# A macaron transformer block on one core: the order of head and tail, and where the softmax sums are scaled

## The chip, the cores and the metric

The kernel runs on one core of a Trainium2 chip. A core has five engines that work through their own instruction queues in order and wait for each other by semaphores: TensorE (PE, matrix products; the rows PEld are its weight loads), VectorE (DVE), ScalarE (ACT), GpSimd (POOL) and SyncE (SP, which here issues nearly all transfers). Matrix products write to PSUM, a small memory that VectorE and ScalarE read; everything else lies in SBUF. The metric is the device time of one execution in microseconds; of several executions the median counts.

## The reference

The input x has 4 batches of 4096 rows of 512 numbers, which makes 128 tiles of 128 rows. The block computes

```python
x = x + 0.5 * ffn(layernorm(x))
x = x + attention(layernorm(x))
x = x + 0.5 * ffn(layernorm(x))
```

ffn rounds both its input and its weight, in blocks of 32 numbers, to a six-bit grid with one scale for each block, multiplies them and adds a bias. attention is a neighbourhood attention with 16 heads of 32 numbers: each query looks at the 13 nearest keys of its sequence, with a relative position bias; the scores go through a softmax, the probabilities are multiplied with the values, and a last product (proj) follows.

## The kernel before, in words

Products are made in a split form, since fp32 operands are written as a high and a low half in fp16. One product of a 128-row tile is 12 matrix instructions of 512 columns (high times low, low times high, high times high, each over four chunks of 128; `product`, L146). In TensorE's rows the products go by the PSUM tile that they fill: pmf is a feed-forward product (two for each tile of rows, f1 and f2), pmv the values, pmqk the queries and keys (two for each item), pmo the product behind the attention. ps are the scores and pv the attention's product with the values, both many small instructions. All 128-row products share three PSUM buffers (`ps_m`, L93), so that a product can start only when the buffer of the third one before it has been read out.

An attention item is one of 128: four groups of 128 channels for each of 32 groups of 512 rows (GROUP is 4 tiles). `project_qk` makes the item's queries and keys: ScalarE writes the high halves (L369), VectorE the low halves (L373). `softmax` (L417 to L486) is a chain over three engines. VectorE adds bias and parts of the scores (L458, L461) and takes the maximum (L465), GpSimd subtracts it (L467), ScalarE takes the exponent (L469), and VectorE sums it for each query and block (L472, tile total, 16 to 18 numbers in each partition), inverts the sum (L473) and multiplies it by the constant PS = 1024 (L474; the second operand p_scale is a tile that holds 1024 everywhere). GpSimd multiplies the exponents by it (L476), ScalarE writes the high half of the probabilities p (L480, L481), GpSimd the low half (L483), and SP issues a transposing transfer into pT (L485). `attend` multiplies with the values, and ScalarE and VectorE empty pv into a ring of 1024 rows (L530, L536), with 1/PS.

A norm with rounding (`quantised_norms`, slots named by their start) is a chain as well: VectorE's statistics (L180, L181), three or four small GpSimd operations for the factors (L186 to L195), ScalarE's yq (L233), VectorE's block maxima, scale and inversion (sc, r; L239 to L244), GpSimd's multiplication (L246), ScalarE's rounding (L249), GpSimd's multiplication back (L251), ScalarE's and VectorE's halves hlq (L200, L204), and a transposing transfer into xT (L205), which the feed-forward product reads. In the long middle part one norm holds two tiles, one for f1 and one for f2; at both ends it holds one. The attention's norm (n2) has a shorter chain with hln and x2. A group's pmqk needs x2 of all its four tiles.

The order of the main part is written out by hand. Every piece of work is a Python generator that is put into a numbered slot with a rank; `run_slot` takes the pieces of a slot by rank, lets each emit instructions up to its next `yield n, rank`, and puts it into the slot n later. STEP is 7 slots, one step for each tile and for each item. In each engine's queue the instructions stand in that order. A yield of 0 would put a piece into the slot that is being run, which the loop before doesn't look at again. The setup ahead of `manual_schedule` (L769) is ordered by the framework's own scheduler instead: the load and rounding of the feed-forward weight fw, the sums of squares of the other weights, and the first EARLY norms. The 16 chunks of the qkv and proj weights (rows, 0 to 11 and 12 to 15) are then scaled, split (`put_scaled`, whl, L774 and L776) and transposed into wt (L699), one chunk every two slots from slot -9 on.

At the end `out_slot` and `second_slot` give the slots of pmo and of the second feed-forward product for the last tiles (LAST is 123). GpSimd adds the biases (`add_bias`, L565); of the last five tiles VectorE adds half of the ffn bias for those with even numbers.

Of the kernel before, what the change touches and what calls it, by code (L numbers as in the profile page):

```python
# [26 lines left out]
F32 = mybir.dt.float32  # L27
# [5 lines left out]
ALU = mybir.AluOpType  # L33
# [4 lines left out]
P = 128  # L38
# [9 lines left out]
MAXB = 18  # L48
# [11 lines left out]
PS = 1024.0  # L60
# [4 lines left out]
def macaron_kernel(  # L65
# [12 lines left out]
    nc = tc.nc  # L78
# [12 lines left out]
    const = ctx.enter_context(tc.tile_pool(name="const", bufs=1))  # L91
# [18 lines left out]

    least = const.tile([P, 2 * NB], F32, name="least")
    nc.vector.memset(least, F8_SCALE * XS * Q_EPS)
    p_scale = const.tile([P, MAXB], F32, name="p_scale")
    nc.vector.memset(p_scale, PS)
    minus_half = const.tile([P, 2], F32, name="minus_half")
    nc.gpsimd.memset(minus_half, -0.5)

# [2 lines left out]
    half_ffn_b = const.tile([P, dim], F32, name="half_ffn_b")  # L120
# [39 lines left out]
    slots = {}  # L160

    def begin(slot, stage, rank=5):
        slots.setdefault(slot, []).append((rank, stage))

    def run_slot(slot):
        for _, stage in sorted(slots.pop(slot, ()), key=lambda e: e[0]):
            for n, rank in stage:
                begin(slot + n, stage, rank)
                break

    xs, ys = {}, {}

# [41 lines left out]
    def moments(slot, t, which):  # L214
        tiles, mv = together[slot]
        if not mv:
            mv.append(sm.tile([P, 2, 2], F32, tag="mv", bufs=4, name=f"mv{slot}"))
        statistics(t, which, mv[0][:, tiles.index((t, which)), :])
# [114 lines left out]
    for g in range(NG):  # L333
        first = done
# [6 lines left out]
    n_items = n_batch * NG * KC  # L341
# [75 lines left out]
    def softmax(m):  # L417

        b, g, c = item_of(m)
        j0, j1 = group_blocks[g]  # L420
        n = j1 - j0
        t = qk.pop(m)


        ps = ps_s.tile([P, 3, 2, 256], F32, tag="s", name=f"ps{m}")
        for i in range(n):
            q0, k0 = (KN + at - g * GT for at in span(j0 + i))
            q0 -= late(j0 + i)
            u, w = divmod(i, PSB)
            for part, sides in ((0, 2), (1, 1)):  # L430
                for h in range(4):
                    rows = slice(h * D, (h + 1) * D)
                    nc.tensor.matmul(  # L433
                        ps[rows, u, :sides, w * KN : (w + 1) * KN],
                        t[rows, 0, part, q0 : q0 + QR], t[rows, 1, :sides, k0 : k0 + KN],
                        start=part == 0, stop=part == 1,
                    )

        def pieces(i, e):

            while i < e:
                u, w = divmod(i, PSB)
                whole = max((e - i) // PSB, 1) if w == 0 else 1
                f = min(e, (u + whole) * PSB)
                yield slice(u, u + whole), slice(w, w + (f - i) // whole)
                i = f

        yield 1, 9
        sf = sfp.tile([P, MAXB, KN], F32, tag="sf", name=f"sf{m}")
        s4 = sf.rearrange("p (u w) k -> p u w k", w=PSB)  # L450
        p4 = ps[:, :, :, : PSB * KN].rearrange("p u a (w k) -> p a u w k", k=KN)
        first = 1 if kind(j0) == 1 else 0
        last = n - (1 if kind(j1 - 1) == 2 else 0)
        for i, e in ((0, first), (first, last), (last, n)):
            for u, w in pieces(i, e):
                o = s4[:, u, w, :]
                bias = table[:, kind(j0 + i), c, :].unsqueeze(1).unsqueeze(1).to_broadcast(o.shape)
                nc.vector.tensor_tensor(o, p4[:, 0, u, w, :], bias, ALU.add)  # L458
        for u, w in pieces(0, n):
            o = s4[:, u, w, :]  # L460
            nc.vector.tensor_tensor(o, o, p4[:, 1, u, w, :], ALU.add)  # L461
        yield 1, 2
        s = sf[:, :n, :]
        top = sm.tile([P, MAXB], F32, tag="top", name=f"top{m}")
        nc.vector.tensor_reduce(top[:, :n], s, AX.X, ALU.max)  # L465
        yield 1, 4
        nc.gpsimd.tensor_tensor(s, s, bc(top[:, :n], KN), ALU.subtract)  # L467
        yield 1, 9
        nc.scalar.activation(s, s, AF.Exp, scale=alpha)  # L469
        yield 1, 4  # L470
        total = sm.tile([P, MAXB], F32, tag="total", name=f"total{m}")
        nc.vector.tensor_reduce(total[:, :n], s, AX.X, ALU.add)  # L472
        nc.vector.reciprocal(total[:, :n], total[:, :n])  # L473
        nc.vector.tensor_tensor(total[:, :n], total[:, :n], p_scale[:, :n], ALU.mult)  # L474
        yield 1, 4
        nc.gpsimd.tensor_tensor(s, s, bc(total[:, :n], KN), ALU.mult)  # L476
        yield 2, 8
        p = p_tile
        ph = p[:, :n, :KN]
        nc.scalar.copy(ph, s)  # L480
        nc.scalar.copy(p[:, :n, 2 * KN : KV], ph)  # L481
        yield 2, 4
        nc.gpsimd.tensor_tensor(p[:, :n, KN : 2 * KN], s, ph, ALU.subtract)  # L483
        pT = ptp.tile([P, MAXB, P], F16, tag="pT", name=f"pT{m}")
        nc.sync.dma_start_transpose(out=pT[:, :n, :], in_=p[:, :n, :].rearrange("p n k -> p (n k)"))  # L485
        probs[m] = pT  # L486
# [68 lines left out]
        nc.sync.dma_start(out=of[t * P : (t + 1) * P, :], in_=xs.pop(t))  # L555


    EARLY = 2
    STEP = 7

    F1, V, QK, SC, PV, OUT, F2 = 5, 2 * STEP + 6, 5 * STEP + 3, 6 * STEP, 8 * STEP + 3, 13 * STEP + 2, 12

    def add_bias(t, b, idle=True):
        engine = nc.gpsimd if idle else nc.vector
        engine.tensor_tensor(xs[t], xs[t], b, ALU.add)  # L565

    def one(f, *args):
        f(*args)
        return
        yield  # L570

    LAST = NT - GROUP - 1

    def out_slot(t):


        i = t - LAST
        if i >= 0:
            return (n_items - 1) * STEP + PV + 3 + i
        if i >= 1 - GROUP:  # L580
            return LAST * STEP + PV + 21 + 4 * i
        return t * STEP + OUT

    def second_slot(t):

        i = t - LAST
        if i in (-2, -1):
            return out_slot(NT - 1) + 3 + i
        return out_slot(t) + (F2 + 2 if i == -3 else F2)

    for t in range(NT):
        k = t * STEP
        begin(k - 18, one(load, t), 0)
        enlist(k - 10, t, "n1")
        if not 0 < t < EARLY:
            begin(k - 11, one(moments, k - 10, t, "n1"), 1)
        begin(k + F1, first_half(t))
        begin(k + V, values(t))
        begin(k + F1, one(add_bias, t, half_ffn_b), 8)
        at = out_slot(t)  # L600
        begin(at - 5, one(add_bias, t, after_b), 8)
        enlist(at + 2, t, "n3")
        begin(at, project_out(t, at + 2))
        begin(at + 6, one(add_bias, t, half_ffn_b, t < LAST or t % 2), 8)
        begin(second_slot(t), second_half(t))
    for slot in together:
        if slot >= EARLY * STEP - 10:
# [6 lines left out]
    for n in range(n_batch * NG):  # L614
        k = n * GROUP * STEP
        b, g = divmod(n, NG)
# [4 lines left out]
    with tc.tile_pool(name="setup", bufs=1) as sp, tc.tile_pool(name="scratch", bufs=2) as scr:  # L621
# [13 lines left out]

        sq = sp.tile([P, 5 * KC], F32, name="sq")
        first = min(slots)
        for slot in range(first, first + 2 * STEP, STEP):
            run_slot(slot)
        for t in range(EARLY):  # L640
            if t:
                moments(t * STEP - 10, t, "n1")
            for _ in quantised_norms(t * STEP - 10):
                pass
        chunks = (8, 9, 10, 11, 0, 4, 1, 5, 2, 6, 3, 7, 12, 13, 14, 15)
        for o in chunks:
            w, i = (qkv_w, o) if o < 3 * KC else (proj_w, o - 3 * KC)
            rows[o] = xp.tile([P, dim], F32, tag="x", name=f"rows{o}")
# [91 lines left out]
        for o in range(KC):  # L740
# [23 lines left out]
            nc.vector.tensor_tensor(hl[:, 1, :], fw[:, o, :], hl[:, 0, :], ALU.subtract)  # L764
            put_weights(4 * KC + o, hl)

        ctx.enter_context(tc.manual_schedule())  # L769

        def put_scaled(o):
            s = up[:, o // KC : o // KC + 1]
            hl = scr.tile([P, 2, dim], F16, tag="whl", bufs=4, name=f"whl{o}")
            nc.scalar.activation(hl[:, 0, :], rows[o], AF.Copy, scale=s)  # L774
            yield 1, 9
            nc.vector.scalar_tensor_tensor(  # L776
                hl[:, 1, :], rows[o], s, hl[:, 0, :], ALU.mult, ALU.subtract
            )
            put_weights(o, hl)
# [23 lines left out]
        def attention_bias():  # L803

            vbx = sp.tile([P, 2, KC, P], F16, name="vbx")
            nc.scalar.copy(vbx[:, 0], bc(vb, P))
            nc.vector.tensor_tensor(vbx[:, 1], bc(vb, P), vbx[:, 0], ALU.subtract)
            yield 1, 9
            pmb = ps_m.tile([P, dim], F32, tag="mm", name="pmb")
            product(pmb, lambda s, c: vbx[:, s, c, :], lambda s, c: wt[:, s, c, PO : PO + dim])  # L810
            yield 1, 9
            nc.vector.scalar_tensor_tensor(after_b, pmb, cp, after_b, ALU.mult, ALU.add)
# [39 lines left out]
                    masks[:, k : k + 1, :].to_broadcast([P, KC, KN]), ALU.mult, ALU.add,  # L852
                )

        begin(-11, one(scales), 9)
        for i, o in enumerate(chunks):
            begin(-9 + 2 * i, put_scaled(o), 9)
        begin(28, attention_bias(), 9)
        begin(26, one(put_table), 9)
        slot = first  # L860
# [48 lines left out]
```

## Time and profile before

| | us |
|---|---|
| runs, median of three | 2447.3 (2446.6, 2447.3, 2453.3) |
| profiled execution, own time | 2451.5 |
| its span, first to last instruction | 2449.7 |

| stretch of the span, us | PE busy | DVE busy | ACT busy | POOL busy | granted PE clock |
|---|---|---|---|---|---|
| 0 to 106 | 32.8 | 81.2 | 50.3 | 58.7 | 0.89 |
| 106 to 240 | 124.4 | 109.9 | 75.3 | 97.6 | 0.96 |
| 240 to 2300 | 2027.9 | 1754.6 | 1143.7 | 1736.1 | 1.00 |
| 2300 to 2400 | 80.8 | 66.6 | 40.9 | 69.3 | 0.92 |
| 2400 to 2450 | 35.4 | 28.4 | 11.6 | 25.4 | 0.84 |

The profile is of one execution. Its page gives busy times of the engines, the chain of work that ended last, and groups of equal instructions with their mean duration and the idle time ahead of them. The trace behind it can be asked for all waits, for the chain piece by piece, and for an engine's instructions in order of time. A row in order of time has the start, the duration from the first of its instructions to the end of the last, engine, line, operation, the written tile, the read tiles, and in brackets the idle time ahead with what ended it. A wait that is shorter than what TensorE has in its pipeline doesn't show as idle time; it shows as a larger distance from one start to the next.

### The profile page before, as it was taken

How to read it: one execution, taken by the hardware profiler on the slowest of the kernel's cores; microseconds unless marked ns; L12 is line 12 of the kernel's file. 1: busy time of each engine (PE TensorE's matmuls, PEld its weight loads, DVE VectorE, ACT ScalarE, POOL GpSimd, SP SyncE). 2: the span in 40 equal slices, each digit the busy share in tenths (PEclk: the TensorE clock that was granted, in tenths of full speed). 3: DMA queues.
4: the chain of work that ended last, by engine and by line, in shares of the span. 5: the costliest groups of instructions: out<-in, count | busy, mean ns of one | idle time of the engine just before them, and what ended most of it. 6: DMA issues, size and time to landing. Idle time of an engine off the chain costs nothing.

```text
span 2449.7 us, 82398 instructions
## 1 busy us (share of the span) xinstructions
PE 2301.3 (94%) x35539; PEld 1114.2 (45%) x35539; DVE 2040.6 (83%) x3590; ACT 1321.7 (54%) x2080; POOL 1987.1 (81%) x2010
## 2 busy tenths in 40 slices
PE   1699999999999999999999999999999999999976
PEld 0244444444444444444444444444444444444432
DVE  7788888888888888888888888888888888888765
ACT  4455555555555555555555555555555555555442
POOL 5677888888888888888888888888888888888665
PEclk9899999999999999999999999999999999999998
DMA  6687888777787778778877778786877877776653
GB/s 165 133 148 143 154 160 157 145 155 145 145 156 155 150 143 158 148 147 156 154 147 156 147 146 156 156 151 145 160 146 149 159 150 153 146 156 127 134 106 83
DMA packets 925702, 360.60 MB, mean 147 GB/s; under 512 B 718876, under 2 KB 889752, under 8 KB 925336
## 3 DMA queue, kind: packets, MB, share of 16 engines
q1 hardware_dynamic: 924992, 354.79, 74.3%
q8 instruction: 278, 4.55, 0.8%
q14 instruction: 88, 0.72, 0.1%
q10 hardware_dynamic: 344, 0.53, 0.1%
HBM read 110.15 MB, written 67.29 MB: 72 GB/s over the span
## 4 chain that ended last, share of the span: by engine, by line
PE 67%; DVE 17%; ACT 8%; DMA 4%; issue 3%; POOL 2%; SPq 0%; POOLq 0%; DVEq 0%; ACTq 0%
PE pmf L151 17%; PE pmqk L151 16%; PE pmo L151 12%; PE pmv L151 12%; PE ps L433 6%; DVE total L474 4%; DVE total L472 3%; PE pv L503 3%; DMA xT<-hlq 3%; ACT sf L469 3%; DVE qk L373 2%; ACT qk L369 2%; ACT ring L530 1%; DVE stn L180 1%; DVE total L473 1%
## 5 line engine op out<-in xcount | busy, mean ns | idle before, releaser
L151 PE MATMUL pmf<-wt,xT 128*128 128x512 f16 x3048 | 706.0, 382 | 41.0 <-DMA xT<-hlq 38.8
L151 PE MATMUL pmqk<-x,wt 128*128 128x512 f16 x3072 | 710.6, 381 | 7.9 <-DMA x<-hln 5.9
L151 PEld LDWEIGHTS <-xT 128*128 128x128 f16 x3048 | 297.6, 98 | 412.2 <-DMA xT<-hlq 53.7
L151 PEld LDWEIGHTS <-wt 128*128 128x128 f16 x3072 | 290.4, 98 | 347.1 <-issue 14.0
L246 POOL TENSOR_TENSOR yq<-yq,r 128x1024 f32<-128x1024 f32 (+1 forms) x141 | 246.3, 1747 | 201.9 <-DVE r L244 199.1
L151 PE MATMUL pmv<-wt,x 128*128 128x512 f16 x1536 | 352.4, 379 | 17.5 <-DVE qk L373 12.8
L151 PE MATMUL pmo<-wt,ring 128*128 128x512 f16 x1536 | 357.7, 383 | 4.3 <-issue 4.2
L310 ACT CAST vt<-pmv 128x512 f16<-128x512 f32 x128 | 74.9, 585 | 471.4 <-PE pmv L151 471.4
L565 POOL TENSOR_TENSOR x<-x,half_ffn_b 128x512 f32<-128x512 f32 x254 | 324.6, 1278 | 0.0
L275 DVE SCALAR_TENSOR_TENSOR x<-pmf,coef,x 128x512 f32<-128x512 f32 x256 | 179.6, 702 | 135.2 <-PE pmf L151 135.1
L530 ACT ACTIVATE ring<-pv 128x510 f16<-128x510 f32 (+8 forms) x224 | 82.3, 414 | 376.1 <-PE pv L503 376.1
L180 DVE BATCH_NORM_STATS2 stn<-x 128x6 f32<-128x512 f32 x384 | 265.3, 691 | 8.7
L151 PEld LDWEIGHTS <-x 128*128 128x128 f16 x1536 | 149.7, 97 | 215.3 <-issue 45.3
L251 POOL TENSOR_TENSOR yq<-q,sc 128x1024 f32<-128x1024 fp8e4 (+1 forms) x141 | 246.2, 1746 | 1.4 <-ACT q L249 1.4
L249 ACT ACTIVATE q<-yq,nudge 128x1024 fp8e4<-128x1024 f32 (+1 forms) x141 | 150.0, 1064 | 143.0 <-POOL yq L246 134.7
L151 PEld LDWEIGHTS <-ring 128*128 128x128 f16 x1536 | 140.9, 98 | 165.0 <-issue 9.7
L233 ACT ACTIVATE yq<-x,nbq,rsq 128x512 f32<-128x512 f32 x254 | 194.4, 809 | 37.7 <-POOL nbq L192 32.3
L476 POOL TENSOR_TENSOR sf<-sf,total 128x714 f32<-128x714 f32 (+2 forms) x128 | 178.6, 1395 | 37.1 <-DVE total L474 36.8
L186 POOL TENSOR_SCALAR rsq<-mv 128x2 f32<-128x2 f32 (+1 forms) x141 | 132.4, 939 | 89.8 <-DVE mv L181 88.4
L467 POOL TENSOR_TENSOR sf<-sf,top 128x714 f32<-128x714 f32 (+2 forms) x128 | 180.8, 1412 | 18.9 <-DVE top L465 18.7
L483 POOL TENSOR_TENSOR p<-sf,p 128x714 f16<-128x714 f32 (+2 forms) x128 | 192.6, 1505 | 4.2 <-ACT p L480 4.2
L458 DVE TENSOR_TENSOR sf<-ps,table 128x210 f32<-128x210 f32 (+5 forms) x288 | 126.5, 486 | 75.6 <-PE ps L433 74.9
(146 smaller groups left out, 3525.5 us busy)
## 6 DMA issues: line engine op xcount, KB each, us to landing
vs<-vd SPq DMA_DIRECT2D x144, 357.0 KB
x<-in_L_attn_x_dram SPq DMA_DIRECT2D x128, 256.0 KB
vd<-vt SPq DMA_DIRECT2D x128, 256.0 KB
out_dram<-x SPq DMA_DIRECT2D x128, 256.0 KB
vs<-vd SPq DMA_DIRECT2D x24, 378.0 KB
vs<-vd SPq DMA_DIRECT2D x24, 315.0 KB
rows<-in_L_attn_qkv_w_dram SPq DMA_DIRECT2D x12, 256.0 KB
xT<-hlq SPq DMA_TRANSPOSE x141
```

Source lines behind the costliest of these rows:

```text
L151: nc.tensor.matmul(pm, lhs(a, c), rhs(b, c), start=(n == 0), stop=(n == 3 * KC - 1))
L180: nc.vector.bn_stats(st, xs[t])
L233: nc.scalar.activation(y[:, u], xs[t], AF.Identity, bias=nb[:, u : u + 1], scale=rs[:, u : u + 1])
L246: nc.gpsimd.tensor_tensor(yb, yb, bc(r, QB), ALU.mult)
L249: nc.scalar.activation(q8, y, AF.Identity, bias=nudge, saturate=False)
L251: nc.gpsimd.tensor_tensor(yb, q8.rearrange("p u (n q) -> p (u n) q", q=QB), bc(sc, QB), ALU.mult)
L275: nc.vector.scalar_tensor_tensor(xs[t], pm, cf, xs[t], ALU.mult, ALU.add)
L433: nc.tensor.matmul(ps[rows, u, :sides, w * KN : (w + 1) * KN], t[rows, 0, part, q0 : q0 + QR], t[rows, 1, :sides, k0 : k0 + KN], start=par ...
L467: nc.gpsimd.tensor_tensor(s, s, bc(top[:, :n], KN), ALU.subtract)
L476: nc.gpsimd.tensor_tensor(s, s, bc(total[:, :n], KN), ALU.mult)
L483: nc.gpsimd.tensor_tensor(p[:, :n, KN : 2 * KN], s, ph, ALU.subtract)
L565: engine.tensor_tensor(xs[t], xs[t], b, ALU.add)
```

## The change

In the softmax, p_scale and L474 go. ScalarE multiplies total by 1/1024 right behind the sum, and VectorE inverts that. The sum comes three ranks earlier in its slot, and the inversion follows at rank 9 of the same slot, by a yield of 0, for which `run_slot` now runs a slot until nothing is left in it. In VectorE's queue the order sum, inversion, multiplication, low half of the queries, low half of the keys becomes sum, low half of the queries, inversion, low half of the keys. In ScalarE's queue the scaling stands between the two yq of the norm and the high half of the keys.

At the start three norms instead of two are made in the setup, and the second and third behind the feed-forward weight's code; the proj weights (12 to 15) come before those of the queries and keys, and the chunks' slots are spread over 2 to 35; the product for the attention's bias (pmb) comes two slots later.

At the end the last five pmo stand two slots apart instead of one, the second products of tiles 119 and 120 move behind the attention product of item 126, the ffn bias of the last five tiles is always GpSimd's and stands two slots ahead of its product.

```diff
-    p_scale = const.tile([P, MAXB], F32, name="p_scale")
-    nc.vector.memset(p_scale, PS)
...
     def run_slot(slot):
-        for _, stage in sorted(slots.pop(slot, ()), key=lambda e: e[0]):
-            for n, rank in stage:
-                begin(slot + n, stage, rank)
-                break
+        while slot in slots:
+            for _, stage in sorted(slots.pop(slot), key=lambda e: e[0]):
+                for n, rank in stage:
+                    begin(slot + n, stage, rank)
+                    break
...
         nc.scalar.activation(s, s, AF.Exp, scale=alpha)
-        yield 1, 4
+        yield 1, 1
         total = sm.tile([P, MAXB], F32, tag="total", name=f"total{m}")
         nc.vector.tensor_reduce(total[:, :n], s, AX.X, ALU.add)
+        nc.scalar.mul(total[:, :n], total[:, :n], 1.0 / PS)
+        yield 0, 9
         nc.vector.reciprocal(total[:, :n], total[:, :n])
-        nc.vector.tensor_tensor(total[:, :n], total[:, :n], p_scale[:, :n], ALU.mult)
         yield 1, 4
...
-    EARLY = 2
+    EARLY = 3
...
-    def add_bias(t, b, idle=True):
-        engine = nc.gpsimd if idle else nc.vector
-        engine.tensor_tensor(xs[t], xs[t], b, ALU.add)
+    def add_bias(t, b):
+        nc.gpsimd.tensor_tensor(xs[t], xs[t], b, ALU.add)
...
         if i >= 0:
-            return (n_items - 1) * STEP + PV + 3 + i
+            return (n_items - 1) * STEP + PV + 3 + 2 * i
...
         i = t - LAST
+        if i in (-4, -3):
+            return (n_items - 1) * STEP + PV + i
         if i in (-2, -1):
             return out_slot(NT - 1) + 3 + i
-        return out_slot(t) + (F2 + 2 if i == -3 else F2)
+        return out_slot(t) + F2
...
-        begin(at + 6, one(add_bias, t, half_ffn_b, t < LAST or t % 2), 8)
+        begin(at + 6 if t < LAST else second_slot(t) - 2, one(add_bias, t, half_ffn_b), 8)
...
-        for slot in range(first, first + 2 * STEP, STEP):
+        for slot in range(first, first + EARLY * STEP, STEP):
             run_slot(slot)
-        for t in range(EARLY):
-            if t:
-                moments(t * STEP - 10, t, "n1")
-            for _ in quantised_norms(t * STEP - 10):
-                pass
-        chunks = (8, 9, 10, 11, 0, 4, 1, 5, 2, 6, 3, 7, 12, 13, 14, 15)
+        for _ in quantised_norms(-10):
+            pass
+        chunks = (8, 9, 10, 11, 12, 13, 14, 15, 0, 4, 1, 5, 2, 6, 3, 7)
...
+        for t in range(1, EARLY):
+            moments(t * STEP - 10, t, "n1")
+            for _ in quantised_norms(t * STEP - 10):
+                pass
...
-            yield 1, 9
+            yield 3, 9
             pmb = ps_m.tile([P, dim], F32, tag="mm", name="pmb")
...
-        begin(-11, one(scales), 9)
-        for i, o in enumerate(chunks):
-            begin(-9 + 2 * i, put_scaled(o), 9)
+        begin(0, one(scales), 9)
+        for slot, o in zip((2, 4, 5, 6, 10, 13, 16, 19, 21, 23, 25, 27, 29, 31, 33, 35), chunks):
+            begin(slot, put_scaled(o), 9)
```

## The prediction

> **What bounds the kernel now.** I read the page's busy shares and chain first, then the chain of waits in one repeating step, then the engines' own rows in time, then the two ends.
>
> ```profile
> PE 2301.3 (94%) x35539; PEld 1114.2 (45%) x35539; DVE 2040.6 (83%) x3590; ACT 1321.7 (54%) x2080; POOL 1987.1 (81%) x2010
> ```
>
> TensorE is busy 94% of 2449.7 us. In the stretch 240 to 2300 us it is busy 2027.9 of 2060 us, so at most 32 us lie there; in 0 to 106 it is busy 32.8 and in 2300 to 2450 116.2. What a faster VectorE is worth is bounded by these idle spaces, not by the work that VectorE is spared. One step in the chain of waits (start, us, what):
>
> ```profile
> 1016.45 0.58 ACT ring L530
> 1017.03 0.58 ACT qk L369
> 1017.61 0.22 ACT qk L382
> 1017.83 0.80 ACT sf L469
> 1018.62 0.02 issue
> 1018.65 0.91 DVE total L472
> 1019.56 0.02 issue
> 1019.58 0.28 DVE total L473
> 1019.86 0.02 issue
> 1019.88 1.12 DVE total L474
> 1021.00 0.67 DVE qk L373
> 1021.67 0.04 issue
> 1021.71 2.75 PE pmv L151 x12
> ```
>
> This is a loop across engines: the attention product pv ends, ScalarE empties it and takes the exponent, VectorE sums, inverts and scales by 1024 (L472 to L474), and only then writes the low half of q (L373), which frees the PSUM buffer for pmv. L474 handles 17 numbers per partition and takes 1.12 us. TensorE's rows in time show what this costs:
>
> ```profile
> 1018.82 2.75 PE L151 MATMUL pmf<-wt,xT 128*128 128x512 f16 x12
> 1021.71 2.75 PE L151 MATMUL pmv<-wt,x 128*128 128x512 f16 x12
> 1024.30 2.75 PE L151 MATMUL pmf<-wt,xT 128*128 128x512 f16 x12
> ```
>
> Without a wait a product starts 2.59 us after the one before it (pmv to pmf here); pmf to pmv is 2.89. Over the 110 steps of the trace that show pmf, pmv, pmf, ps whole, the distances over 2.59 add to 30.4 us for pmf to pmv and to 9.0 for pmv to the second pmf, which waits for the transposed tile xT. Nothing else repeats. The waits view, with less because it counts only full idleness, agrees in kind (us, times, longest):
>
> ```profile
> PE pmf L151 <- DMA xT<-hlq: 38.8, 17, 14.3
> ...
> PE pmv L151 <- DVE qk L373: 12.8, 57, 0.7
> ```
>
> The ends, in TensorE's rows:
>
> ```profile
> 73.79 5.30 PE L151 MATMUL pmf<-wt,xT 128*128 128x512 f16 x12 [14.31 <-DMA xT<-hlq]
> ```
> ```profile
> 2415.03 5.34 PE L151 MATMUL pmf<-wt,xT 128*128 128x512 f16 x24
> 2430.72 15.05 PE L151 MATMUL pmf<-wt,xT 128*128 128x512 f16 x60 [10.35 <-DMA xT<-hlq]
> ```
>
> **The scaling of the sums.** Removed: 128 of L474, 174 to 1302 ns, median 1124. In the quoted step it began at 1019.88 and ended as GpSimd's bias add (1019.70 + 1.27 = 20.97) ended. Added: 128 ScalarE scalings of 16 to 18 columns; the nearest row, ring 128x16, takes 191 ns. In the instruction order ScalarE runs it behind the two yq (end 1020.06) and ahead of the second high half of q, which thus moves by about 0.2 us: 1020.3 to 1020.95. VectorE now runs the sum, then the first low half at once (1019.58 to 1020.25 instead of from 1021.00), then waits about 0.1 for ScalarE, inverts (0.27), and takes the second low half from 1020.95 to 1021.65 instead of 1022.33. The first frees pmv's buffer 1.4 us earlier, 1.1 before pmf has ended; the second frees the next pmf's 2.4 before it is wanted. GpSimd's multiplication by total, which waits behind the inversion, could start at 1020.65, but GpSimd is in its bias add to 1020.97 anyway. The wait of 0.3 is gone; what is late next is xT. Its issue stands on SP behind pT's. In 17 of the 110 steps the second pmf already waits for xT (every fourth step, where a pT issue takes 4.5 to 6 us behind the stack loads vs); these steps hold 5.2 of the 30.4, and that is lost again. In some eight more xT has less than 0.35 to spare; half of their 2.6 goes. So 30.4 - 5.2 - 1.3 = 24 gained. Ends: 0, if every step then waits for xT, and 30.4 + 9.0 = 39, if pT's issue, held by GpSimd's p, also moves forward by the 0.7 that VectorE gains. I take 24, as 93 of 110 steps show no wait for xT at all.
>
> [...]
>
> **The head.** Tile 2's norm moves from the slots into the setup: VectorE gets statistics, maximum, scale and inversion ahead of the last FFN weight (0.69 + 0.18 + 0.67 + 0.2 + 0.25 = 2.0), GpSimd the factors, tile 0's bias (1.26) and a multiplication (1.05). VectorE is busy 23.3 of 25 us there, so I let the first pmf move from 52.8 to 56 (ends: 53 and 58). x2 and x3 are loaded before the transposes, which cost SP 0.6 each, hidden. Tile 2's xT (SP issue 1.23) now follows the first whl at about 55 and is there before pmf of tile 1 ends, so the gap of 14.31 goes: that pmf runs at 62.5 instead of 73.8. This is not the gain, since the next tile's norm is a chain of its own: in before, hlq of one tile to hlq of the next (68.7, 78.4, 88.4) takes about 10 us. From tile 0's add (60 instead of 61.6; VectorE is free of five whl by then) I add statistics, three GpSimd factors, yq, maximum, two multiplications, q, hlq twice: hlq of tile 4 ends near 83 to 84 instead of 89.1. The attention bias changes little: pmb stands between the same products and still waits for vbx (95.4 before, some 92 now, behind one more whl of 1.2); but VectorE's after_b, which stood 3.69 idle for pmb ahead of the next hlq, now comes behind it. The eight whl moved to slots 19 to 35 each put 0.72 on ScalarE, 0.7 to 1.25 on VectorE and 1.2 to 1.8 of SP issue into these steps, three or four a step as the steps before them had. Together the first pmqk goes from 105.8 to about 101: 5 gained. Ends: 4 lost (the setup's 3.2, and one whl more on the path), 10 gained (a whole norm step). I take 5, from the nearest rows. From 106 on TensorE is the limit again, and the delay carries over one to one.
>
> **The tail.** Before, GpSimd works through the factors of four tiles, each held by pmo's 2.59, before the first multiplication (yq at 2415.71, though its factor r was ready at 2412.9); the five xT issue from 2427.95 and five pmf follow from 2430.72. After the change GpSimd's order alternates: factors 123, bias 127, factors 124, yq 123, factors 125, and so on. Counted from 2406.74 with the rows' durations (five factor chains of 1.2, ten multiplications of 1.05, four biases of 1.27): 6 + 10.5 + 5.1 = 21.6, so the last multiplication ends near 2428.5 instead of 2433.8. The two biases that leave VectorE (1.5 each) come last on GpSimd, by 2431, before their pmf ends. hlq (0.62 + 1.05) and the 2.8 from xT's issue to its product (as from 2427.95) put the last pmf at 2433.0; its 2.6, the add 0.75 and the 3.1 from add to end give 2439.5: 10.2 gained. SP alternates xT with the outputs; an xT that waits there behind an output waits for a product already done by 2427.5. Lost: the last ring write stands behind one more add (0.67), and in the last items, where GpSimd does wait for total (2.31 at 2333, 2.67 at 2353) and L474 took only 0.18, the ScalarE hop and the low half in front cost up to 0.48 each, thrice: 2.1 together. Moving the products of tiles 119 and 120 behind pv of item 126 is costed at nothing: pv of item 127 waits for pT (5.34), whose issue GpSimd's p releases at 2394.6. Without that cover a product of 2.6 would show. So 8 gained; ends 0 and 12 (the whole gap of 10.35, and the 2.1 by which 15.05 exceeds 60 times 0.216).
>
> [...]
>
> **Sum.** 24 + 5 + 8 = 37. The profiled execution took 2451.5 (span 2449.7); 2451.5 - 37 = 2414.5. It stood 4.2 above the median of the runs, 2447.3, so I forecast 2410.
>
> **Rivals.** First, the wait only changes its name: xT, not q, ends last in most steps, since it comes by SP after pT. For it: in the chain view xT appears between steps about every 72 us. Against: 93 steps have no such wait, and half the steps have 7.5 us or more between xT's issue and its product where the late ones have 5.2. Then 24 shrinks to about 6: 2428. Second, the head loses: the added setup work and the denser whl make the early norm steps longer, and 4 is lost instead of 5 gained: 2419; for it the setup's VectorE share, against it the 14.31 gap. Third, slower: the new ScalarE hop is put where the scaling was short. Place: total between L472 and GpSimd's L476; price 0.48 a step, 128 steps, 61 us, less 13 from the ends: 2495. It decides if GpSimd, not TensorE, sets the step, that is if its idle time ahead of yq (1.67 in the step shown, waiting for r) falls to nothing. GpSimd is busy 81%; 1.67 a step speaks against it. Fourth, the removed operation was covered and the ends cancel: 2445 to 2450, against the 2.89 of pmf to pmv.
>
> **How the numbers follow.** Runs tell about 0.3% (7.3 us) from no change. Forecast 0.60 (its own range 2399 to 2420), xT 0.17, head 0.12, slower 0.06, covered 0.05. Faster: 0.60 + 0.16 + 0.12 = 0.88; same 0.06; slower 0.06. The range reaches down to 2398, where xT's 9 us come too (39 instead of 24), and up to 2434, past the xT case with a head that gains nothing; beyond lie the last two cases and a few hundredths at either end.
>
> **What would show it.** L474 gone, a 0.2 us ScalarE row on total; pmf to pmv at 2.59 in most steps and VectorE no releaser of pmv; xT's wait not above some 15 us between 240 and 2300; TensorE idle there near 8 to 10 instead of 32. The third pmf follows the second without a gap, the first pmqk near 101. The last run of five pmf broken up, the end some 9 us nearer to the last pmo than before (34.5: 2415.2 to 2449.7). I am wrong if pmv to pmf grows as pmf to pmv shrinks, if the first pmf starts past 58, or if SP holds the last xT behind an output.

## The result, and the profile after

The changed kernel takes 2461.4 us in the median (2454.0 to 2470.7, 12 runs), the kernel before 2448.6 on the same chip (2443.1 to 2453.3, 12 runs). The ratio is 1.0053, with a 95% interval of 1.004 to 1.0066: slower by 0.5%, where 2410 and a gain of 1.5% had been forecast. The profiled execution of the changed kernel took 2455.8 us, its span is 2454.0. The changed file has other line numbers: L149 is the matrix product (L151 before), L471 the sum, L472 ScalarE's scaling, L474 the inversion, L372 the low halves.

The page's busy shares of the changed kernel come first:

```profile
PE 2294.5 (94%) x35539; PEld 1116.3 (45%) x35539; DVE 1939.6 (79%) x3459; ACT 1333.7 (54%) x2208; POOL 1984.7 (81%) x2012
```

VectorE is spared 101 us, ScalarE has 128 instructions and 12 us more. The removed part itself went as forecast. VectorE's, ScalarE's and TensorE's rows in time of one step (start, us, engine, line, operation, tiles, and in brackets the idle time ahead):

```profile
1023.07 0.90 DVE L471 TENSOR_REDUCE total<-sf 128x17 f32<-128x714 f32 x1 [0.64 <-ACT sf L468]
1023.89 0.74 DVE L372 SCALAR_TENSOR_TENSOR qk<-pmqk,qk_b,qk 128x512 f16<-128x512 f32 x1
1024.62 0.27 DVE L474 RECIPROCAL total<-total 128x17 f32<-128x17 f32 x1
```
```profile
1024.39 0.20 ACT L472 ACTIVATE total<-total 128x17 f32<-128x17 f32 x1
```
```profile
1023.24 2.75 PE L149 MATMUL pmf<-wt,xT 128*128 128x512 f16 x12
1025.83 2.75 PE L149 MATMUL pmv<-wt,x 128*128 128x512 f16 x12
```

The low half stands ahead of the inversion, the scaling takes 0.20, and pmv starts 2.59 after pmf, the distance without a wait. Summed from 340 to 2300 us, the time over 2.59 between pmf and pmv falls from 29.5 us to 0.0. But TensorE's waits (us in total, times, longest) and its busy time by stage show it spent elsewhere:

```profile
PE pmf L149 <- DMA xT<-hlq: 33.8, 26, 4.3
...
PE pv L503 <- DMA pT<-p: 12.9, 2, 7.3
PE pmqk L149 <- issue: 10.4, 8, 2.4
PE ps L432 <- issue: 10.1, 4, 4.4
PE pv L503 <- issue: 9.4, 9, 1.7
```
```profile
0.00:106.00 106.00, 33.70 (x115) 13.18 (x115) 85.54 (x166) 49.74 (x97) 57.26 (x84) 0.92 0.63 152
...
240.00:2300.00 2060.00, 2011.11 (x31538) 984.28 (x31536) 1647.45 (x2911) 1150.06 (x1877) 1725.38 (x1703) 1.00 0.80 150
```

(In the second fence: stretch, its length, then busy us and instructions of PE, PEld, DVE, ACT and POOL, PE's granted clock, DMA share, GB/s.) Between 240 and 2300 TensorE is now idle for 48.9 us, where it was 32.1. The total of the xT waits looks smaller than before (38.8), but of the old total 14.3 was the gap in the head and 10.4 the one in the tail; from 340 to 2300 alone the waits for xT grew from 4.9 to 19.7. There the time that pmv to the second pmf takes over 2.59 grew from 8.3 to 23.2 us, in 21 steps, the larger ones 72 us apart or a multiple of it, at each fourth step. The other pairs of neighbours grew by another 25 us, most of which the waits call "issue" (7.8 us before, 26.4 now), idle time that waits for nothing the profile shows.

The ends, in TensorE's rows:

```profile
62.76 2.75 PE L149 MATMUL pmf<-wt,xT-3_389 128*128 128x512 f16 x12
65.35 2.75 PE L149 MATMUL pmf<-wt,xT 128*128 128x512 f16 x12
...
106.21 4.04 PE L149 MATMUL pmqk<-x,wt 128*128 128x512 f16 x18 [1.60 <-DMA x<-hln]
```
```profile
2424.93 5.34 PE L149 MATMUL pmf<-wt,xT 128*128 128x512 f16 x24
2430.99 2.76 PE L149 MATMUL pmf<-wt,xT 128*128 128x512 f16 x12 [0.72 <-DMA xT<-hlq]
2435.66 2.76 PE L149 MATMUL pmf<-wt,xT 128*128 128x512 f16 x12 [1.90 <-DMA xT<-hlq]
2440.37 9.63 PE L149 MATMUL pmf<-wt,xT 128*128 128x512 f16 x36 [1.95 <-DMA xT<-hlq]
```

The gap ahead of the third pmf is gone, yet the first pmqk starts at 106.2, as before (105.8). The last five pmf are broken up, and from the last pv to the end it takes 44.8 us (2409.2 to 2454.0) instead of 50.2. What was lost, then, lies in the steady steps.

### The profile page after: what moved, and what is told of

The parts are those of the page before. It is cut to its first block, busy times and chain, and to the rows that moved or that the text cites. A ratio compares the mean times of both kernels' runs of the same rounds, so it can differ in the third digit from the quotient of the medians.

```text
span 2454.0 us, 82265 instructions
## 1 busy us (share of the span) xinstructions
PE 2294.5 (94%) x35539; PEld 1116.3 (45%) x35539; DVE 1939.6 (79%) x3459; ACT 1333.7 (54%) x2208; POOL 1984.7 (81%) x2012
## 4 chain that ended last, share of the span: by engine, by line
PE 81%; DMA 6%; DVE 5%; ACT 3%; issue 3%; POOL 2%; SPq 0%; DVEq 0%; POOLq 0%; ACTq 0%
PE pmqk L149 24%; PE pmf L149 24%; PE pmo L149 13%; PE pmv L149 11%; PE ps L432 6%; DMA xT<-hlq 5%; PE pv L503 3%; ACT yq L232 1%; ACT qk L368 1%; ACT sf L468 1%; DVE stn L179 1%; DVE fw L749 0%; POOL rsq L188 0%; ACT ring L530 0%; DVE sf L457 0%
## 5 line engine op out<-in xcount | busy, mean ns | idle before, releaser
L149 PE MATMUL pmf<-wt,xT 128*128 128x512 f16 x3048 | 705.8, 382 | 33.9 <-DMA xT<-hlq 33.8
L149 PE MATMUL pmqk<-x,wt 128*128 128x512 f16 x3072 | 713.2, 382 | 17.4 <-issue 10.4
L149 PEld LDWEIGHTS <-xT 128*128 128x128 f16 x3048 | 297.2, 98 | 407.9 <-DMA xT<-hlq 49.0
L149 PEld LDWEIGHTS <-wt 128*128 128x128 f16 x3072 | 291.0, 98 | 358.0 <-issue 27.6
L149 PE MATMUL pmo<-wt,ring 128*128 128x512 f16 x1536 | 359.1, 384 | 5.2 <-issue 5.1
L149 PE MATMUL pmv<-wt,x 128*128 128x512 f16 x1536 | 354.9, 381 | 5.1 <-DVE mvn L180 5.1
L149 PEld LDWEIGHTS <-x 128*128 128x128 f16 x1536 | 150.7, 98 | 188.4 <-DMA x<-hln 5.6
L372 DVE SCALAR_TENSOR_TENSOR qk<-pmqk,qk_b,qk 128x512 f16<-128x512 f32 x256 | 190.9, 746 | 43.4 <-ACT qk L368 42.7
L149 PEld LDWEIGHTS <-ring 128*128 128x128 f16 x1536 | 141.1, 98 | 166.4 <-issue 10.6
```

The costliest lines, as they stand in the source:

```text
L149: nc.tensor.matmul(pm, lhs(a, c), rhs(b, c), start=(n == 0), stop=(n == 3 * KC - 1))
L372: nc.vector.scalar_tensor_tensor(t[:, s, 1, KN:], pms[s], bias, t[:, s, 0, KN:], ALU.add, ALU.subtract)
```

## The experiments

Each run is compared with runs of the kernel before on the same chip, so that the time of the kernel before differs a little from group to group. Four runs took the parts one by one and tried the suspect that the trace offered: every fourth step the second pair's stack loads (vs) stand on SP directly ahead of an output, an x load, pT and xT, and there pT's issue took 5.2 us before and 6.3 after.

**The scaling alone** (head and tail of before; `run_slot` as in the change):

```diff
-    p_scale = const.tile([P, MAXB], F32, name="p_scale")
-    nc.vector.memset(p_scale, PS)
...
-        yield 1, 4
+        yield 1, 1
         total = ...
         nc.vector.tensor_reduce(total[:, :n], s, AX.X, ALU.add)
+        nc.scalar.mul(total[:, :n], total[:, :n], 1.0 / PS)
+        yield 0, 9
         nc.vector.reciprocal(total[:, :n], total[:, :n])
-        nc.vector.tensor_tensor(total[:, :n], total[:, :n], p_scale[:, :n], ALU.mult)
```

> The scaling part alone, with head and tail of before. Theory A (the wait for the low halves goes, and its 27 us come back as waits for xT and as instructions that TensorE issues late, because DMA and not VectorE sets the pace of a step): the time is 8 to 14 us over before, 2455 to 2463, with no wait pmv<-DVE qk, pmf<-DMA xT some 25 to 35 us in 340-2300 and over 20 us of idle time that waits for nothing. Theory B (the scaling gains its 24 us and it is the new head that puts the steps out of phase with the transfers): 2420 to 2430, with pmf<-DMA xT near the 17 us of before.

Measured: 2467.9 against 2448.3, ratio 1.0084 (1.0055 to 1.0113). It is slower alone than with the other parts, and theory B, which blamed the head, falls. The time is a little past theory A's range.

**The head alone and the tail alone** (the diff's other two parts).

> The head part alone: three tiles ahead of the loop, the new order of weight chunks, the scales at slot 0. Theory A: the head is worth -4 to +2 us, as the start of the 12th step showed (347.5 to 343.4), so 2443 to 2451, and the steady steps keep the 27 us of pmv<-DVE qk. Theory B: the head alone makes it slower by 20 us or more, 2468 to 2480, with longer waits for xT in 340-2300.

> The tail part alone: the last products out and halves in their new slots. Both theories: nothing changes before 2300 us, and from the last pv to the end 5 us less (50.2 to about 45), so 2443 to 2446. If the new slots of the last outputs hold up SP's queue for the last items, the 2 to 4 us that after lost between items 120 and 127 are in it too, and the time is 2446 to 2450.

Measured: the head 2451.5, ratio 1.0015 (1.0001 to 1.0029), at the upper end of theory A's range; the tail 2445.6, ratio 0.9985 (0.9972 to 0.9998), in the first range. The head gains nothing, the tail some 3 to 4 us.

**The stack loads four slots later, in the changed kernel and in the one before.**

```diff
-        begin(k + 8 * STEP, one(load_stack, b, g, 1), 9)
+        begin(k + 8 * STEP + 4, one(load_stack, b, g, 1), 9)
```

> After, with the loads of the second pair's stack issued four slots later (slot 60 of each group in place of 56), so that they no longer stand on SP ahead of an output, an x load and the transposes pT and xT. Theory A in its narrow form (those loads are what makes xT late): the wait pmf<-DMA xT falls from 33.8 to under 15 us and the time by 15 to 25, to 2431 to 2446. Theory A in its wide form (any transfer's bytes delay the instructions that TensorE fetches): xT's wait falls but issue stalls stay at or above 30 us, and the time is 2446 to 2456. Theory B: no difference from after, 2455 to 2465.

> Before, with only the second pair's stack loads moved from slot 56 to slot 60 of each group. If the collision on SP every fourth step costs the kernel whether or not TensorE waits for VectorE, the 8.2 us of pmv-to-pmf excess in 340-2300 go, the 27 us of pmv<-DVE qk stay, and the time is 2425 to 2440. If it costs only where the scaling has made TensorE arrive earlier, the time is 2444 to 2452.

Measured: changed kernel 2415.1, ratio to before 0.9863 (0.984 to 0.9887); kernel before 2436.8, ratio 0.9949 (0.993 to 0.9967). The first lies below all its ranges, the second in its first range. In the changed kernel pmv to pmf from 340 to 2300 fell from 23.2 to 0.0 us over its 2.59. So those loads are where most of the loss is. At their old place they cost the changed kernel 46 us and the kernel before 11; why four times as much, these runs don't say.

**The order without ScalarE, and another way to free the low half.** In the first the sum, low half and inversion stand in the new order, but the multiplication by p_scale stays on VectorE, behind the inversion (`run_slot` again as in the change). In the second the old kernel's low half goes ahead of the sum:

```diff
-        yield 1, 4
+        yield 1, 1
         total = ...
         nc.vector.tensor_reduce(total[:, :n], s, AX.X, ALU.add)
+        yield 0, 9
         nc.vector.reciprocal(total[:, :n], total[:, :n])
         nc.vector.tensor_tensor(total[:, :n], total[:, :n], p_scale[:, :n], ALU.mult)
```
```diff
-        yield 1, 6
+        yield 1, 3
         put_low(0)
```

> Before, with the order of the scaling part (reduce, low half, reciprocal) but with the multiply kept on VectorE behind the reciprocal and no work for ScalarE. If the order alone frees the low half, pmv<-DVE qk is gone as in the scaling alone and the time is within 6 us of it, 2455 to 2472. If it was the multiply's 0.2 us on VectorE that counted, the wait stays over 15 us and the time is 2444 to 2452.

> Before, with the query's low half put ahead of the reduce of the sums on VectorE and nothing else moved: the wait pmv<-DVE qk goes, but the probabilities and so the transpose pT come 0.5 to 0.8 us later instead of earlier. If any earlier arrival of TensorE is given back at the fourth steps, the time is 2448 to 2468, with pmf<-DMA xT over 25 us in 340-2300. If it is pT's earlier start into the stack loads that costs, as the scaling part brings it, this keeps half or more of the 27 us: 2422 to 2436.

Measured: the order alone 2416.1, ratio 0.9863 (0.9834 to 0.9892), the low half first 2424.1, ratio 0.9887 (0.9864 to 0.991). The first misses both ranges by 28 us and more, and with it theory A in its general form fell: with the wait for the low half gone, the gain was not given back. The second lies in its second range, but the reason given there, that pT's earlier start costs, does not stand: in the mean of the fourth steps pT starts 5.3 us behind the loads in the first, which gains, and in the scaling alone, which loses. What remained between 2416 and 2468 was ScalarE's instruction in place of VectorE's, and the rows of both kernels did not bear that out: VectorE's and GpSimd's work stood at the same places within the step, and pT's issue started at the same moment (9.9 us after pmv in the mean of some 27 fourth steps) but took 6.2 us with ScalarE's scaling and 5.3 without.

**Scaling and tail, without the new head.**

> Scaling and tail without the new head, the stack loads in their old slot 56. If the head of the change is worth -4 to +4 us when the scaling is in too, the time is within 5 us of after, 2453 to 2466. If the new head is what kept after from being slower still (the scaling alone stood at 2468), it is 2462 to 2472.

Measured: 2470.0, ratio 1.0073 (1.0048 to 1.0099), the second range. The new head is not the cause of the loss: without it the kernel is no faster (2470.0 against 2461.4 with it). Whether the 8 us between the two are the head's is not shown, as the intervals of the two ratios overlap.

**What else had gone: the tile.** Every kernel so far that was slower than before by more than 0.3% lacked p_scale; every faster one had it, but for the changed kernel with the later loads. p_scale is 72 bytes in each partition, laid out as 96, near the start of the memory; without it every later tile lies 96 bytes lower. In the built programs of before and after the stack vs starts at 204288 and 204192, that is at 798 times 256 and 96 bytes below it; the x tiles (65792, 65696) and pT (195072, 194976) also left a multiple of 256. Four runs tested this as theory C, against the instruction itself (theory D):

```diff
+    p_scale = const.tile([P, MAXB], F32, name="p_scale")
+    nc.vector.memset(p_scale, PS)
```

in after; the same in after with the later stack loads; the same in the scaling alone; and in the kernel before

```diff
     nc.vector.memset(p_scale, PS)
+    shift = const.tile([P, 40], F32, name="shift")
+    nc.vector.memset(shift, 0.0)
```

> After, with the constant tile p_scale kept in its place, written once and read by nothing. Theory C (taking out those 72 bytes, 96 as they are laid out, moves every later tile 96 bytes down, off the 256-byte boundaries on which x, vs and pT stood, and their transfers take longer): all the loss goes, pT's issue at the fourth steps falls from 6.3 to about 5.3 us, and the time is 2400 to 2418, the forecast of 2410 in it. Theory D (it is ScalarE's hop itself that delays): no difference from after, 2455 to 2465. [...]

> Before, with an unused constant tile of 160 bytes behind p_scale, so that all later tiles lie 160 bytes higher, which is the same place within 256 bytes as 96 lower. Theory C: the transfers lengthen as in after, and before loses what lies beyond its 27 us of waits for VectorE and more, 2465 to 2495, with pT's issue at the fourth steps near 6 us. Theory D: 2444 to 2452.

> After with the tile kept and the second pair's stack loads at slot 60. Theory C: both remove waits for the same transposes, so the gains do not add up; what is left of waits for xT goes, and the time is 2390 to 2410. Theory D: as with the loads moved alone, 2411 to 2419.

> The scaling part alone with the tile kept. Theory C: 24 us under before as forecast for it, give or take 10, 2414 to 2434, against 2468 without the tile. Theory D: 2460 to 2476.

Measured, all against 2446.5 for the kernel before: after with the tile 2407.1, ratio 0.9847 (0.9827 to 0.9866); before shifted 2488.2, ratio 1.0171 (1.0155 to 1.0186); after with the tile and later loads 2389.1, ratio 0.9769 (0.9755 to 0.9783), just under its range; the scaling alone with the tile 2416.5, ratio 0.988 (0.986 to 0.9901). All four went theory C's way; theory D is out. An unused tile of 72 bytes is worth some 50 us in after (54 by the medians, 50 by the ratios, 1.0053 against 0.9847), and 160 unused bytes cost before 42. The later loads are worth 18 us with the tile (2407.1 to 2389.1), against 46 without it. With the loads moved and the tile gone some 25 us are still lost (2415.1 against 2389.1), so the loss is not in that one collision alone. The multiplication on ScalarE (2416.5) is worth no more than the order alone with VectorE's (2416.1).

SP's rows in time of one fourth step, in after and then in after with the tile, from the stack loads to xT:

```profile
1136.72 1.58 SPq L408 DMA_DIRECT2D vs<-vd  x3
1138.40 1.53 SPq L555 DMA_DIRECT2D out_dram<-x  x1
1139.97 0.43 SPq L175 DMA_DIRECT2D x<-in_L_attn_x_dram  x1
1141.92 6.65 SPq L485 DMA_TRANSPOSE pT<-p  x1
1148.67 3.13 SPq L204 DMA_TRANSPOSE xT<-hlq  x1
```
```profile
1116.80 1.57 SPq L410 DMA_DIRECT2D vs<-vd  x3
...
1122.04 5.72 SPq L487 DMA_TRANSPOSE pT<-p  x1
1127.86 3.13 SPq L206 DMA_TRANSPOSE xT<-hlq  x1
```

pT starts 5.2 us behind the stack loads in both, and its issue ends 0.9 later in after (11.85 against 10.96 behind the loads). xT stands behind it. The 5.3 us from the stack loads on, in three such steps of after, then of after with the tile (last two columns: DMA share, GB/s):

```profile
994.14:999.44 5.30, 5.30 (x156) 2.91 (x155) 3.93 (x7) 4.58 (x7) 5.20 (x6) 1.00 0.96 185
1065.74:1071.04 5.30, 5.30 (x156) 2.88 (x155) 3.97 (x7) 4.53 (x7) 5.20 (x6) 1.00 0.91 179
1136.72:1142.02 5.30, 5.30 (x156) 2.90 (x155) 3.94 (x7) 4.58 (x7) 5.20 (x6) 1.00 0.94 180
```
```profile
975.75:981.05 5.30, 5.30 (x156) 2.90 (x155) 3.96 (x7) 4.62 (x7) 5.20 (x6) 1.00 0.96 215
1046.15:1051.45 5.30, 5.30 (x156) 2.88 (x155) 3.97 (x7) 4.65 (x7) 5.20 (x6) 1.00 0.94 216
1116.80:1122.10 5.30, 5.30 (x156) 2.90 (x155) 3.96 (x7) 4.62 (x7) 5.20 (x6) 1.00 0.90 199
```

The DMA engines are as busy and move less. Over 27 such steps the mean is 179 GB/s in after, 205 with the tile, and 204 before, each at a mean DMA share of 0.90, 0.90 and 0.89. The page says the same of the main queue (packets, MB, share of 16 engines), after and then after with the tile:

```profile
q1 hardware_dynamic: 924992, 354.79, 77.0%
```
```profile
q1 hardware_dynamic: 924992, 354.79, 74.7%
```

Of spans of 2454.0 and 2410.4 us these are 1890 and 1801 us for the same packets and bytes.

**Which tile.** Four runs started from after with p_scale kept and took one group of tiles off its place, by unused bytes ahead of it and, where later tiles were to keep their place within 256 bytes, behind it. For the stack the edit is

```diff
+    gap0 = ctx.enter_context(tc.tile_pool(name="gap0", bufs=1))
+    nc.vector.memset(gap0.tile([P, 40], F32, name="gap0t"), 0.0)
     vsp = ctx.enter_context(tc.tile_pool(name="vsp", bufs=2))
```

The others are alike: pT and the tiles between are moved by 160 bytes up. For x, p_scale is left out and 96 unused bytes stand behind the x tiles, so that the constants and x lie 96 bytes lower.

> After without p_scale, but with 96 unused bytes behind the x tiles, so that the constants and the x tiles alone lie 96 bytes lower and every later tile is where it was before. If the x loads and outputs carry the loss (two 256 KB transfers in every step), most of the 54 us between 2407 and 2461 are here: 2440 to 2462. If the stack does: within 8 us of 2407.

> After with the tile kept and the stack vs alone moved 160 bytes up. If the stack's loads carry it (pieces of 512 bytes, the shortest here, and they stand ahead of pT every fourth step): 2435 to 2462. If x does: within 8 us of 2407.

> After with the tile kept and pT alone moved 160 bytes up. If it is the transpose itself that gets longer with its target's place, 2430 to 2460 and longer pT issues in all steps; otherwise within 8 us of 2407.

> After with the tile kept and the tiles between x and pT (split halves, xT, x2, vt, ring, p, qk, sf) moved 160 bytes up; of these xT, vt and p stood on odd multiples of 128 bytes before, not on 256. If a 256-byte boundary is what counts, little changes here: within 8 us of 2407. If 64 or 128 bytes count, or any target of a transpose, 2420 to 2460.

Measured, against 2448.6: x 2411.5, ratio 0.985 (0.9827 to 0.9872); vs 2458.5, ratio 1.0049 (1.0032 to 1.0066); pT 2405.1, ratio 0.9835 (0.9813 to 0.9856); the tiles between 2406.7, ratio 0.9835 (0.9813 to 0.9858). The stack alone carries the loss: its ratio is that of the whole change (1.0053), and the intervals of the other three take in that of nothing moved (0.9847). Its profile repeats that of after, in TensorE's wait for xT and the queue's share:

```profile
PE pmf L151 <- DMA xT<-hlq: 29.0, 23, 5.3
```
```profile
q1 hardware_dynamic: 924992, 354.79, 77.3%
```

**How far.** The same edit with 32 and 64 words in place of 40:

> After with the tile kept and the stack vs moved up by 128 bytes, to an odd multiple of 128. If only whole multiples of 256 bytes are good: as with 160 bytes, 2450 to 2466. If 128 is enough: within 8 us of 2407.

> After with the tile kept and the stack vs moved up by 256 bytes, to the next multiple of 256. If the boundary counts: within 8 us of 2407. If any move of the stack costs: 2450 to 2466.

Measured, against 2449.6: 128 bytes 2445.1, ratio 0.9983 (0.9966 to 1.0), between the two ranges; 256 bytes 2411.9, ratio 0.9845 (0.9826 to 0.9865). A move by 256 costs nothing (0.9845, against 0.9847 with nothing moved), so of the moves tried it is the place within 256 bytes that counts. At 128 about 70% of the loss is there (2445.1 - 2411.9 = 33, against 2458.5 - 2411.9 = 47 at 160), and in the fourth steps the mean rate is 186 GB/s, against 200 at 256 and 179 at 160.

The traces also list every packet that the transfers are made of, with its size and duration. All but a few of the 138 thousand packets of 512 bytes belong to the stack's loads. They are not the shortest in the list: 694 thousand have 256 bytes and take 18 ns in the median in before and after. From 340 to 2300 us those of 512 take 36 to 38 ns in the median in every run whose stack starts on a multiple of 256 bytes, 45 at 128 bytes past one, and 47 or 48 at 160, as in after. The packets of 2048 bytes take 84 in all of these runs, also with x off its place. TensorE reads the stack too, as the weights of pv, but its rows don't change: in before, after, after with the tile and with the stack moved, a weight load of vs takes 93 ns in the median and a matrix instruction of pv 183. So it is the packets of the loads that get longer, not the reading of the tile.

Why a packet takes longer there, no run shows.

## Why the prediction was wrong, point by point

**The step that failed** is "The scaling of the sums", in what it left out. It counted removed, added and moved instructions and their durations, and costed the going of the tile p_scale at nothing, without a word. The going of the tile moved the stack to a place 96 bytes below a multiple of 256, its 512-byte packets took 47 ns instead of 38, and that cost some 50 us (2461.4 against 2407.1 with the tile). None of the rivals held this.

**The sum without it came out, in part by luck.** 37 us were forecast and 2410; with the tile kept it is 2407.1, 39 us under before. But the scaling gained more than forecast and the head and the tail less, and the misses cancel. Term by term, in the trace of the kernel with the tile where no other is named:

- Scaling, 24 forecast: a step takes 17.78 us in the mean of items 12 to 120, against 18.05, which makes 29 us in 108 steps; the scaling alone with the tile is 30 us faster in the median. TensorE's idle time from 240 to 2300 is 17.5 (2060 - 2042.49), forecast 8 to 10.
- What would be late next, xT in the fourth steps: the place (behind the stack loads) was right, the amount was not. The forecast took 6.5 us (5.2 and 1.3) off the 30.4 as given back to xT; pmv to pmf over 2.59 from 340 to 2300 is 5.3 us, against 8.3 before, so nothing was given back, which is most of what the scaling gained beyond 24. The forecast had the loads' duration as fixed, and that is what moved in after.
- Head, 5 forecast: nothing. The first pmqk is at 106.2 in after and 106.6 with the tile (105.8 before), and the head alone does not gain (1.0001 to 1.0029). In after the first pmf came at 58.5, past the 58 named as a sign of error, and the gap of 14.3 did go, but the norms' chain that ends the head did not get shorter: TensorE waits 5.14 for mvn ahead of pmv at 73.2 and 4.29 for xT at 82.8, and pmb still 3.85 for vbx.
- Tail, 8 forecast: 5.4 from the last pv to the end (50.2 to 44.8 in after; 44.3 with the tile), 3 to 4 as measured alone. In after the last run of pmf starts as late behind the last pv as before (31.1 against 31.3 us), after waiting 1.95 for xT; the gain is that it holds three products instead of five (9.63 us against 15.05). GpSimd's last multiplication ended 3.2 us earlier behind the last pv (31.1 against 34.3), where 5.3 had been forecast.

**The rivals.** The wait that changes its name (2428) was in the profile of after, and the sign named for it came: pmv to pmf grew from 8.3 to 23.2 us as pmf to pmv shrank. But the runs with the tile show that xT had room; it was made late by slower loads. The slower case named ScalarE's hop; with and without it the kernel takes the same (2416.5, 2416.1). The covered operation with ends that cancel did not happen. The head that loses came half true: it gained nothing.

**The inversion at its new place** takes 234 to 268 ns in all 128 calls (L474), against 252 to 269 before (L473). The gain is that of the order (2416.1 with VectorE's multiplication, 2416.5 with ScalarE's).

**Left open:** why part of the loss shows as "issue" on TensorE and not as a wait. From 340 to 2300 that time is 26.4 us in after and 10.5 with the tile, so it goes with the slower loads. All 19 of these pauses over 0.1 us in after stand 6 to 12 us behind the start of a stack load. The list of packets has a further hint. The page names one of the DMA queues "instruction" (q8, 278 packets of 16 KB). In all 19 pauses such a packet had started 2.2 to 3.4 us ahead of the moment at which TensorE went on; a moment picked at random has one there in 14 of 100 cases. With the tile it is 12 of 12, before 9 of 9. So TensorE seems to have waited for its next instructions, which came late beside the stack loads. No run changed that fetch, so this is argued and not shown.

The best of these kernels is the changed one with the tile kept and the second pair's loads four slots later: 2389.1 us, 2.3% under before.

## What to carry to other kernels

A diff that removes or adds a tile, however small, moves every tile laid out behind it: compare the tiles' places in both programs as one compares their instructions. Here the stack's packets of 512 bytes took 36 to 38 ns where the stack starts on a multiple of 256 bytes, 45 at 128 past one and 47 or 48 at 160. When a part seems to cost what none of its instructions can explain, run it once with its side effects undone (here, the tile kept and unused) before forming a theory of queues. And try the order without the new instruction: here it held the whole gain of the scaling.

## What the runs showed of the hardware that was not expected

The stack's loads in pieces of 512 bytes, starting 160 bytes past a multiple of 256, took 47 ns a packet instead of 38 and moved 179 GB/s together with their neighbours, against 205 on a multiple, and that cost some 50 us of the whole (2461.4 against 2407.1). Transposes into pT at the same offset (2405.1), and x rows of 2048 bytes (2411.5), stayed within the measurement of 2407.1. At 128 bytes past a multiple the loss was smaller than at 160 (33 and 47 us). In the traces of before, after and after with the tile, from 340 to 2300 us, every pause of TensorE over 0.1 us that the profile puts down to no wait (40 in all) ended 2.2 to 3.4 us behind the start of a 16 KB packet of the instruction queue.
